# An adapter with a chosen expert ahead of a chosen feed-forward: the first block's bias, index reads, norm rows and idle products

## The chip, the cores and the metric

The kernel runs on one core of a Trainium2 chip. The metric is the device time of one execution in microseconds (us). Before the change it is 899.83 us, the median of three runs (899.83, 899.83 and 900.68). Engines are called as the profile calls them: PE is TensorE's matmul, PEld its weight load, DVE is VectorE, ACT is ScalarE, POOL is GpSimd, and SP is the sync engine, which here only reads indices and issues transfers.

## The reference

The input x is 2 sequences of 2048 tokens of width 512, in float32. Each sequence carries one index for each of two layers.

```python
# layer 1: adapter, one of 16 experts per sequence
hidden = gelu(x @ down_W.T + down_b)                 # 512 -> 128
hidden = where(valid, hidden @ expert_W[idx].T + expert_b[idx], hidden)
hidden = hidden + domain_emb[idx]
hidden = hidden @ up_W.T + up_b                      # 128 -> 512
x = layernorm(hidden + x) * ln_gamma + ln_beta
# layer 2: feed-forward, one of 8 experts per sequence
h = gelu(x @ Wi[e] + bi[e])                          # 512 -> 2048
x = layernorm(h @ Wo[e] + bo[e] + x) * gamma[e] + beta[e]
```

Nothing nonlinear stands between the chosen expert and the up projection, so the kernel folds the two matrices into one, and the three biases that follow the first gelu into one row of 512 values: `up_W @ (valid * expert_b + domain_emb) + up_b`.

## The kernel before, in words

The tokens are cut into 8 blocks of 512 (four per sequence), a block into four sub-tiles of 128 tokens; x lies in SBUF with tokens on the 128 partitions. For each block the adapter gives the normalized x and its transpose `yT`, `f_in` multiplies by Wi (2048 columns in four stages `d`) and applies gelu, and `f_out` multiplies by Wo, adds the residual and normalizes. Both large products are done in seven half-size products instead of eight (`mul` calls with sums of blocks that POOL and DVE prepare); only the very first stage of the first block, `pC`, is done plainly, in two halves, so that it can start when half of `yT` is there.

Every engine executes its instructions in the order in which the Python code writes them. There is no scheduler: later blocks' adapter work is put between products through hooks (`F` for `f_in`, numbered 0 to 27, and `G` for `f_out`), while the first block's adapter is written out by hand ahead of the loop (L668 to L706). A PSUM tile comes from small pools; the adapter's pieces share two "aux" buffers, so a piece must wait until what lies in its buffer has been read.

The parts that the change touches are these.

- L106 to L125: the first loads. SP issues the two index vectors and x's sub-tiles 0 and 1; ACT issues `down_W`, x's sub-tiles 2 and 3, `down_b`, `up_W`, and then three rows that are each copied to all 128 partitions: `up_b`, `ln_gamma`, `ln_beta`. The transfers of SP and ACT take eight semaphores in turn, and one that takes a semaphore again waits at its issue until the transfer that had it before has landed.
- L150 to L151: SP reads both sequences' indices for both layers, four reads, before it issues anything that uses one (`load_expert`, `load_wi` and the rest, L654 to L663).
- `fold_expert`, `fold_up`, `fold_bias`: the folding for a sequence. `fold_up` also makes `biasx`, the expert's bias vector repeated 128 times, by a product with ones and a copy by ACT. For the first block the bias comes in two parts: `a_residual(0)` lets POOL add `up_b` to x, and `a_up` adds `biasx` times the up projection by a second matmul into the same PSUM tile. For all other blocks `fold_bias` makes a full 128x512 tile of the whole bias once per sequence, and POOL adds it to x.
- L674: nine products of ones with ones (`keep_busy`) at the very start, into a PSUM tile that nobody reads.
- L682 to L706: the first block's order: all four transposes of x, two down projections, the transpose of up_W, the third down projection, the folding, the fourth, then `a_up` for sub-tiles 0 and 1, `a_norm`, the transpose of the expert's `bi`, `a_up` for 2 and 3, and the transposes into `yT` (`a_out`) for 0 and 1. `second_half` (L708) does the rest between the two halves of `pC`.
- L746 to L750: the second sequence's folding, at hooks 10, 17, 22 and 23 of the block before it.

Of the kernel before, what the change touches and what calls it, by code (L numbers as in the profile page):

```python
# [17 lines left out]
def kernel(  # L18
# [34 lines left out]
    P = 128  # L53
# [32 lines left out]
    def aux(name, pool=None, tag="aux"):  # L86
        return (pool or ps_a).tile([P, 512], F32, tag=tag, name=name)
# [24 lines left out]
    db = cpool.tile([A, 1], F32, name="db")  # L112
    g0 = cpool.tile([P, D], F32, name="g0")
    b0 = cpool.tile([P, D], F32, name="b0")
    upb = cpool.tile([P, D], F32, name="upb")
    nc.sync.dma_start(x_tiles[0][:, 0, :], xr[0][:, 0, :])
    nc.scalar.dma_start(dW, down_W)
    nc.sync.dma_start(x_tiles[0][:, 1, :], xr[0][:, 1, :])
# [1 line left out]
    nc.scalar.dma_start(x_tiles[0][:, 3, :], xr[0][:, 3, :])  # L120
    nc.scalar.dma_start(db, down_b.rearrange("(a o) -> a o", o=1))
    nc.scalar.dma_start(uW, up_W.rearrange("(c p) a -> p c a", p=P))
    nc.scalar.dma_start(upb, up_b.partition_broadcast(P))
    nc.scalar.dma_start(g0, ln_gamma.partition_broadcast(P))
    nc.scalar.dma_start(b0, ln_beta.partition_broadcast(P))  # L125

    ident = cpool.tile([P, P], F32, name="ident")
    make_identity(nc, ident)
    mhalf = cpool.tile([P, NS], F32, name="mhalf")
    nc.gpsimd.memset(mhalf, -0.5)  # L130

    tok_f = cpool.tile([1, 2, B], F32, name="tok_f")
    nc.vector.tensor_copy(tok_f, tok_i)
# [13 lines left out]
    flags = cpool.tile([1, 2, B], F32, name="flags")  # L147
    nc.vector.scalar_tensor_tensor(flags[:, 0, :], tok_f[:, 0, :], 0.0, below, ALU.is_ge, ALU.mult)
    nc.vector.tensor_scalar(flags[:, 1, :], flags[:, 0, :], -1.0, 1.0, ALU.mult, ALU.add)
    e0 = [nc.sync.value_load(e_i[0:1, 0, b : b + 1], min_val=0, max_val=E0 - 1) for b in range(B)]  # L150
    e1 = [nc.sync.value_load(e_i[0:1, 1, b : b + 1], min_val=0, max_val=E1 - 1) for b in range(B)]  # L151


    seq = [{} for _ in range(B)]
# [1 line left out]
    def load_expert(b):  # L156
        w = seq[b]
        w["eb"] = spool.tile([1, 2, A], F32, tag="eb", name=f"eb_{b}")
        nc.sync.dma_start(w["eb"][:, 0, :], expert_b[ds(e0[b], 1)])
        nc.sync.dma_start(w["eb"][:, 1, :], domain_emb[ds(e0[b], 1)])  # L160
        w["ew"] = spool.tile([A, A], F32, tag="ew", name=f"ew_{b}")
        nc.sync.dma_start(w["ew"], expert_W[ds(e0[b], 1)].rearrange("e o a -> (e o) a"))
# [11 lines left out]
    def fold_expert(b):  # L174

        w = seq[b]
        v, iv = flags_all[:, 0, b : b + 1], flags_all[:, 1, b : b + 1]
        row = spool.tile([1, A], F32, tag="ebias", name=f"ebias_{b}")
        nc.vector.scalar_tensor_tensor(row, w["eb"][:, 0, :], flags[:, 0, b : b + 1], w["eb"][:, 1, :], ALU.mult, ALU.add)

        eff = spool.tile([A, A], F32, tag="eff", name=f"eff_{b}")
        nc.vector.tensor_scalar(eff, ident, iv, None, ALU.mult)
        nc.vector.scalar_tensor_tensor(eff, w["ew"], v, eff, ALU.mult, ALU.add)
        w["ebias"], w["eff"] = row, eff

    def fold_up(b):
        w = seq[b]
        pw = aux(f"pw_{b}")
        nc.tensor.matmul(pw, w["eff"], uWT, start=True, stop=True)
        w["up"] = spool.tile([A, D], F32, tag="up", name=f"up_{b}")  # L190
        nc.scalar.copy(w["up"], pw)

        pe = aux(f"pe_{b}")
        nc.tensor.matmul(pe[:, :P], w["ebias"], ones[0:1, :], start=True, stop=True)
        w["biasx"] = spool.tile([A, P], F32, tag="biasx", name=f"biasx_{b}")
        nc.scalar.copy(w["biasx"], pe[:, :P])

    def fold_bias(b):
        w = seq[b]
        pb = aux(f"pb_{b}")  # L200
        nc.tensor.matmul(pb, w["biasx"], uWT, start=True, stop=False)
        nc.tensor.matmul(pb, ones[0:1, :], upb[0:1, :], start=False, stop=True)
        w["upb"] = spool.tile([P, D], F32, tag="upb", name=f"upb_{b}")
        nc.scalar.copy(w["upb"], pb)

# [10 lines left out]
    def load_wi(n, d):  # L216
        b = n // BPB
        t = wi_pool.tile([P, NC, 2, 2 * P], F32, tag="wi", name=f"wi_{n}_{d}")
        src = Wi[ds(e1[b], 1)].rearrange("e (c p) (r i) -> p (e c) r i", p=P, r=2)
        for r in range(2):  # L220
            nc.sync.dma_start(t[:, :, r, :], src[:, :, r, d * 2 * P : (d + 1) * 2 * P])
        wi_tiles[n, d] = [t]
# [71 lines left out]
    def a_transpose(n, s):  # L294
        if s == 0:
            live["xT"] = t_pool.tile([P, NC, TB], F32, tag="xyT", name=f"xT_{n}")
        transpose_subtile(x_tiles[n][:, s, :], live["xT"], s, f"x_{n}_{s}", n == 0)

    def a_down(n, lo, hi):

        xT = live["xT"]
        if lo == 0:
            live["hid"] = t_pool.tile([A, TB], F32, tag="hid", name=f"hid_{n}")
        t = slice(lo * P, hi * P)
        if n == 0:
            ph = aux(f"pdown_{n}_{lo}", *((ps_y, "Y") if lo % 2 else (ps_w, "W")))
        else:
            ph = aux(f"pdown_{n}")
        for c in range(NC):
            nc.tensor.matmul(ph[:, t], dWT[:, c, :], xT[:, c, t], start=(c == 0), stop=(c == NC - 1))  # L310
        nc.scalar.activation(live["hid"][:, t], ph[:, t], AF.Gelu, bias=db, scale=1.0)

    def a_residual(n):


        by = seq[n // BPB]["upb"] if n else upb
        for s in range(NS):
            nc.gpsimd.tensor_tensor(x_tiles[n][:, s, :], x_tiles[n][:, s, :], by, ALU.add)

    def a_up(n, s):  # L320
        w = seq[n // BPB]
        pu = aux(f"pup_{n}_{s}")
        nc.tensor.matmul(pu, live["hid"][:, ts(s, P)], w["up"], start=True, stop=(n > 0))  # L323
        if n == 0:
            nc.tensor.matmul(pu, w["biasx"], uWT, start=False, stop=True)
        r = x_tiles[n][:, s, :]
        nc.vector.tensor_add(r, pu, r)
        if s == 0:
            live["mv"] = moments_tile(f"a_{n}")
        moments(live["mv"], s, r, f"a_{n}_{s}")  # L330
        if n == 0:
            live["rstd", s] = rstds(live["mv"], s, s + 1, EPS0, f"a_{n}_{s}")
        elif s % 2:
            live["rstd", s] = live["rstd", s - 1] = rstds(live["mv"], s - 1, s + 1, EPS0, f"a_{n}_{s}")

    def a_norm(n, s):
        normalize(x_tiles[n][:, s, :], live["mv"], live["rstd", s], s, g0, b0)
# [313 lines left out]
        nc.sync.dma_start(outr[n][:, s, :], x_tiles[n][:, s, :])  # L651


    load_expert(0)  # L654
    load_wi(0, 0)
    load_bi(0)
    load_wi(0, 1)
# [21 lines left out]
    for c in range(NC):  # L679
        nc.tensor.transpose(pd[:, ts(c, P)], dW[:, ts(c, P)], ident)  # L680
    nc.vector.tensor_copy(dWT.rearrange("p c a -> p (c a)"), pd)
    for s in range(NS):  # L682
        a_transpose(0, s)
    a_residual(0)
    a_down(0, 0, 1)
    a_down(0, 1, 2)
    pu = aux("pt_uW")
    for c in range(NC):
        nc.tensor.transpose(pu[:, ts(c, P)], uW[:, c, :], ident)
# [2 lines left out]
    fold_expert(0)  # L692
    fold_up(0)
    a_down(0, 3, 4)
    a_up(0, 0)
    a_up(0, 1)
    a_norm(0, 0)
    fold_bi(0)
    a_norm(0, 1)
    a_up(0, 2)  # L700
    a_up(0, 3)
    sums_wi(0, 1)
    a_out(0, 0)
    a_out(0, 1)
    a_norm(0, 2)
    a_norm(0, 3)  # L706

# [13 lines left out]
    for n in range(NB):  # L721
        b, k = divmod(n, BPB)
        fresh = k == 0
        F = {i: [] for i in range(28)}
        for d in range(ND):
            if m := after(n, d, 3):
                F[7 * d + 6].append(lambda m=m: load_wi(*m))
            if m := after(n, d, 2):
                F[7 * d + 6].append(lambda m=m: sums_wi(*m))
        if fresh:  # L730
            for i in range(4):
                F[7 * i + 5].append(lambda i=i: sums_wo(b, i))
        if fresh and n:
            F[0].append(lambda: load_wo(b))
        if n:
            for s, i in enumerate((0, 1, 3, 4)):
                F[i].append(lambda s=s: f_moments(n - 1, s))
            F[4].append(lambda: f_rstd(n - 1, 0, NS))
            for s, i in enumerate((7, 8, 14, 15)):
                F[i].append(lambda s=s: f_normalize(n - 1, s))  # L740
                F[i + 3].append(lambda s=s: f_store(n - 1, s))
            if n + 1 < NB:
                F[19].append(lambda: load_x(n + 1))
            if fresh:
                F[19].append(lambda: (load_row(b, "gamma", gamma), load_row(b, "beta", beta)))
        if k == BPB - 1 and b + 1 < B:  # L746
            F[10].append(lambda: (load_expert(b + 1), load_bi(b + 1), load_row(b + 1, "bo", bo)))
            F[17].append(lambda: fold_expert(b + 1))
            F[22].append(lambda: fold_up(b + 1))
            F[23].append(lambda: fold_bias(b + 1))  # L750
        for d in range(ND - 1):
            F[7 * (d + 1) + 3].append(lambda d=d: h_s13(n, d))
        f_in(n, F)
        G = adapter_pieces(n + 1) if n + 1 < NB else {}
        if k == BPB - 1 and b + 1 < B:
            G[2].append(lambda: fold_bi(b + 1))
        f_out(n, G, n + 1 == NB)
# [34 lines left out]
```

## Time and profile before

| what | value |
|---|---|
| median of three runs | 899.83 us |
| the profiled execution: its time, its span | 902.11 us, 900.34 us |
| PE busy, share of the span | 883.6 us, 98% |
| PEld, DVE, ACT, POOL busy | 83%, 54%, 25%, 38% |
| mean granted TensorE clock | 0.993 |
| first product of `pC` starts | 33.82 us |
| last product ends | 893.83 us |
| moved from HBM | 53.37 MB read, 8.39 MB written |

The profile is of one execution, which took 2.28 us longer than the median; 1.77 us of its time lie outside the span of its instructions. Times in the views are microseconds from the start of the span. A row of the timeline has the start, the busy time, the engine, the line in the code, the operation with what it writes and reads, and in brackets the engine's idle time before it with what ended that. A row of the view by stretches has the stretch, then its length, each engine's busy time in it (with the number of instructions), the granted clock as a share of full speed, the busy share of the 16 transfer engines and the rate in GB/s. The chain of waits is followed back from the last instruction, and its time-ordered form lists the start, the time and the work.

### The profile page before, as it was taken

To read this page: it belongs to the slowest core of one execution; us is meant where nothing else is said; L and a number is where in the kernel's file an instruction comes from. 1 tells how busy PE (TensorE), PEld (TensorE's weight loads), DVE (VectorE), ACT (ScalarE), POOL (GpSimd) and SP (SyncE) were. 2 spreads that over 40 slices of the span, in tenths; PEclk is the share of its full clock that TensorE was granted. 3 is DMA by queue.
4 is the path that set the end of the run, shared out by engine and by line. 5 is a ranking of instruction groups with operands and counts; after the bars stand their busy time and mean duration, and the time that the engine had idled before them with its cause. 6 is when DMAs were issued, how large, how long until landed. Compare 5 with 4: busy or idle time off the path is not lost.

```text
span 900.3 us, 10433 instructions
## 1 busy us (share of the span) xinstructions
PE 883.6 (98%) x4054; PEld 747.2 (83%) x4054; DVE 485.0 (54%) x689; ACT 225.3 (25%) x463; POOL 339.7 (38%) x255
## 2 busy tenths in 40 slices
PE   7899999999999999999999999999999999999997
PEld 6588888887888878888788888888888887888876
DVE  2644374743657446663556746465374843556235
ACT  2134201431034301343013520144101540034200
POOL 2588511542224512344026970244411552224001
PEclk8899999999999999999999999999999999999999
DMA  9622100340013300251007610034000440011001
GB/s 269 248 87 67 36 0 1 129 152 1 1 46 122 113 1 1 66 183 48 1 1 257 187 47 1 1 117 142 22 1 1 140 141 1 0 47 47 1 1 47
DMA packets 46860, 62.42 MB, mean 69 GB/s; under 512 B 2360, under 2 KB 35932, under 8 KB 45916
## 3 DMA queue, kind: packets, MB, share of 16 engines
q1 hardware_dynamic: 45276, 59.93, 19.6%
q10 hardware_dynamic: 1536, 1.84, 0.8%
q8 instruction: 32, 0.52, 0.2%
q14 instruction: 16, 0.13, 0.1%
HBM read 53.37 MB, written 8.39 MB: 69 GB/s over the span
## 4 chain that ended last, share of the span: by engine, by line
PE 94%; DVE 1%; issue 1%; ACT 0%; POOLq 0%; POOL 0%; DVEq 0%; ACTq 0%
PE gX L384 18%; PE pX L384 18%; PE pZ L384 12%; PE gZ L384 12%; PE gW L384 6%; PE pW L384 6%; PE pY L384 6%; PE gY L384 6%; PE pdown L310 3%; PE pup L323 3%; PE pC L384 2%; PE pt_y L291 2%; PE pt_x L291 1%; DVE x L541 0%; DVE x L279 0%
## 5 line engine op out<-in xcount | busy, mean ns | idle before, releaser
L404 ACT ACTIVATE h<-c,biT 128x256 f32<-128x256 f32 x248 | 105.8, 497 | 76.4 <-DVE c L451 76.4
L384 PE MATMUL gX<-wo,h 128*128 128x256 f32 x512 | 115.6, 379 | 1.7 <-DVE x L541 1.7
L384 PE MATMUL pX<-yT,wi 128*128 128x256 f32 x496 | 117.2, 379 | 0.0
L384 PEld LDWEIGHTS gX<-wo,h 128*128 128x128 f32 x512 | 95.6, 190 | 14.1 <-DVE x L541 2.1
L384 PEld LDWEIGHTS pX<-yT,wi 128*128 128x128 f32 x496 | 94.2, 190 | 12.8
L447 ACT COPY c<-pX 128x512 f32<-128x512 f32 x93 | 54.0, 580 | 182.1 <-PE pX L384 182.1
L230 POOL TENSOR_TENSOR wis<-wi 128x512 f32<-128x512 f32 x31 | 41.2, 1329 | 131.7 <-PE pZ L384 131.7
L274 POOL TENSOR_TENSOR rstd_a<-ve_a,mhalf 128x2 f32<-128x2 f32 (+1 forms) x18 | 16.0, 887 | 186.2 <-DVE ve_a L272 186.2
L451 DVE TENSOR_TENSOR c<-pX,c 128x512 f32<-128x512 f32 x31 | 21.4, 691 | 112.0 <-ACT c L447 112.0
L292 ACT COPY yT<-pt_y 128x512 f32<-128x512 f32 x32 | 18.7, 587 | 225.2 <-PE pt_y L291 225.2
L541 DVE TENSOR_TENSOR x<-gX,x 128x512 f32<-128x512 f32 x32 | 21.4, 689 | 99.6 <-PE gX L384 99.5
L274 POOL TENSOR_TENSOR rstd_f<-ve_f,mhalf 128x4 f32<-128x4 f32 (+2 forms) x10 | 10.2, 1024 | 155.6 <-DVE ve_f L272 155.6
L508 DVE TENSOR_TENSOR s<-s,h 128x512 f32<-128x512 f32 x32 | 35.6, 1154 | 47.9 <-PE gZ L384 47.9
L347 POOL TENSOR_TENSOR x<-x,bo 128x512 f32<-128x512 f32 x32 | 41.0, 1284 | 53.2 <-PE pt_y L291 53.2
L384 PEld LDWEIGHTS gX<-wos,s 128*128 128x128 f32 x256 | 48.6, 190 | 13.2 <-issue 6.7
L384 PE MATMUL pZ<-yTs,wis 128*128 128x256 f32 x248 | 58.7, 379 | 0.0
L384 PE MATMUL pX<-yTs,wis 128*128 128x256 f32 x248 | 58.7, 379 | 0.0
L384 PEld LDWEIGHTS gZ<-wos,s 128*128 128x128 f32 x256 | 48.6, 190 | 12.1 <-issue 6.2
L384 PE MATMUL pW<-yTs,wi 128*128 128x256 f32 x248 | 58.6, 379 | 0.0
L384 PE MATMUL pY<-yT,wi 128*128 128x256 f32 x248 | 58.6, 379 | 0.0
L384 PE MATMUL pZ<-yT,wis 128*128 128x256 f32 x248 | 58.6, 379 | 0.0
L384 PE MATMUL gX<-wos,s 128*128 128x256 f32 x256 | 57.8, 379 | 0.3 <-DVE x L541 0.3
(114 smaller groups left out, 1541.4 us busy)
## 6 DMA issues: line engine op xcount, KB each, us to landing
wi<-in_L_cond_Wi_dram SPq DMA_DIRECT2D x64, 512.0 KB, 4.3
wo<-in_L_cond_Wo_dram SPq DMA_DIRECT2D x16, 512.0 KB, 10.0
out_dram<-x SPq DMA_DIRECT2D x32, 256.0 KB, 2.0
x<-in_x_dram SPq DMA_DIRECT2D x7, 1024.0 KB, 4.9
x<-in_x_dram SPq DMA_DIRECT2D x2, 256.0 KB, 4.0
x<-in_x_dram ACTq DMA_DIRECT2D x2, 256.0 KB, 5.1
bo<-in_L_cond_bo_dram SPq DMA_DIRECT2D x2, 256.0 KB, 7.6
gamma<-in_L_cond_gamma_dram SPq DMA_DIRECT2D x2, 256.0 KB
```

What stands on the lines that cost most here:

```text
L230: tt(s1, a21, a22, ALU.add)
L274: nc.gpsimd.tensor_tensor(rstd[:, lo:hi], ve[:, lo:hi], mhalf[:, lo:hi], ALU.pow)
L291: nc.tensor.transpose(pt[:, ts(c, P)], src[:, ts(c, P)], ident)
L310: nc.tensor.matmul(ph[:, t], dWT[:, c, :], xT[:, c, t], start=(c == 0), stop=(c == NC - 1))
L323: nc.tensor.matmul(pu, live["hid"][:, ts(s, P)], w["up"], start=True, stop=(n > 0))
L347: nc.gpsimd.tensor_tensor(r, r, seq[n // BPB]["bo"], ALU.add)
L384: nc.tensor.matmul(bank[:, q], lhsT(k, q), rhs(k, q), start=first, stop=True, skip_group_check=True)
L404: nc.scalar.activation(h[:, j, c * HT : (c + 1) * HT], pre[:, q], AF.Gelu, bias=w["bi"][:, j : j + 1], scale=1.0)
L447: nc.scalar.copy(t, src)
L451: nc.vector.tensor_add(t, src, t)
L508: nc.vector.tensor_tensor(t[:, i : i + 2], s1[:, i : i + 2], h_blocks(n, k, k + 2)[0], ALU.subtract)
L541: nc.vector.tensor_add(t, src, t)
```

## The change

`up_b` is loaded as one row of 512 values instead of 128 copies, and it, `ln_gamma` and `ln_beta` are issued from POOL's queue after its first memsets instead of from ACT's. SP reads one index at a time: the first sequence's adapter index, then its three adapter loads, then its feed-forward index; the second sequence's two reads move to hook 10.

The whole bias becomes one row. `fold_up` makes a column of the expert's bias (a matmul with one output column, copied by DVE), the new `fold_row` multiplies it by the up projection into one row of PSUM and DVE adds `up_b`. In the first block `a_up` adds that row by a matmul with ones instead of the `biasx` product, and POOL's four adds of `a_residual(0)` are gone. `fold_bias` spreads the row to 128 partitions by one matmul instead of two.

In the first block's order the transposes of x are mixed with the down projections, the transpose of `bi` moves behind `a_up` of sub-tile 3, and `keep_busy` products are put in at four places (6, 6, 2 and 2).

```diff
-    upb = cpool.tile([P, D], F32, name="upb")
+    upb = cpool.tile([1, D], F32, name="upb")
...
-    nc.scalar.dma_start(upb, up_b.partition_broadcast(P))
-    nc.scalar.dma_start(g0, ln_gamma.partition_broadcast(P))
-    nc.scalar.dma_start(b0, ln_beta.partition_broadcast(P))
-
     ident = cpool.tile([P, P], F32, name="ident")
     make_identity(nc, ident)
     mhalf = cpool.tile([P, NS], F32, name="mhalf")
     nc.gpsimd.memset(mhalf, -0.5)
+    nc.gpsimd.dma_start(upb, up_b.rearrange("(o d) -> o d", o=1))
+    nc.gpsimd.dma_start(g0, ln_gamma.partition_broadcast(P))
+    nc.gpsimd.dma_start(b0, ln_beta.partition_broadcast(P))
...
-    e0 = [nc.sync.value_load(e_i[0:1, 0, b : b + 1], min_val=0, max_val=E0 - 1) for b in range(B)]
-    e1 = [nc.sync.value_load(e_i[0:1, 1, b : b + 1], min_val=0, max_val=E1 - 1) for b in range(B)]
+    e0, e1 = {}, {}
+
+    def read_e0(b):
+        e0[b] = nc.sync.value_load(e_i[0:1, 0, b : b + 1], min_val=0, max_val=E0 - 1)
+
+    def read_e1(b):
+        e1[b] = nc.sync.value_load(e_i[0:1, 1, b : b + 1], min_val=0, max_val=E1 - 1)
...
-        row = spool.tile([1, A], F32, tag="ebias", name=f"ebias_{b}")
-        nc.vector.scalar_tensor_tensor(row, w["eb"][:, 0, :], flags[:, 0, b : b + 1], w["eb"][:, 1, :], ALU.mult, ALU.add)
         eff = spool.tile([A, A], F32, tag="eff", name=f"eff_{b}")
         nc.vector.tensor_scalar(eff, ident, iv, None, ALU.mult)
         nc.vector.scalar_tensor_tensor(eff, w["ew"], v, eff, ALU.mult, ALU.add)
+        row = spool.tile([1, A], F32, tag="ebias", name=f"ebias_{b}")
+        nc.vector.scalar_tensor_tensor(row, w["eb"][:, 0, :], flags[:, 0, b : b + 1], w["eb"][:, 1, :], ALU.mult, ALU.add)
...
         pe = aux(f"pe_{b}")
-        nc.tensor.matmul(pe[:, :P], w["ebias"], ones[0:1, :], start=True, stop=True)
-        w["biasx"] = spool.tile([A, P], F32, tag="biasx", name=f"biasx_{b}")
-        nc.scalar.copy(w["biasx"], pe[:, :P])
+        nc.tensor.matmul(pe[:, 0:1], w["ebias"], ones[0:1, 0:1], start=True, stop=True)
+        col = spool.tile([A, 1], F32, tag="ecol", name=f"ecol_{b}")
+        nc.vector.tensor_copy(col, pe[:, 0:1])
+        w["ecol"] = col
+
+    def fold_row(b):
+
+        w = seq[b]
+        pb = aux(f"pb_{b}")
+        nc.tensor.matmul(pb[0:1, :], w["ecol"], uWT, start=True, stop=True)
+        w["brow"] = spool.tile([1, D], F32, tag="brow", name=f"brow_{b}")
+        nc.vector.tensor_add(w["brow"], pb[0:1, :], upb)
 
     def fold_bias(b):
         w = seq[b]
-        pb = aux(f"pb_{b}")
-        nc.tensor.matmul(pb, w["biasx"], uWT, start=True, stop=False)
-        nc.tensor.matmul(pb, ones[0:1, :], upb[0:1, :], start=False, stop=True)
+        pb = aux(f"pbb_{b}")
+        nc.tensor.matmul(pb, ones[0:1, :], w["brow"], start=True, stop=True)
...
     def a_residual(n):
 
-
-        by = seq[n // BPB]["upb"] if n else upb
         for s in range(NS):
-            nc.gpsimd.tensor_tensor(x_tiles[n][:, s, :], x_tiles[n][:, s, :], by, ALU.add)
+            nc.gpsimd.tensor_tensor(x_tiles[n][:, s, :], x_tiles[n][:, s, :], seq[n // BPB]["upb"], ALU.add)
...
         if n == 0:
-            nc.tensor.matmul(pu, w["biasx"], uWT, start=False, stop=True)
+            nc.tensor.matmul(pu, ones[0:1, :], w["brow"], start=False, stop=True)
...
+    read_e0(0)
     load_expert(0)
+    read_e1(0)
     load_wi(0, 0)
...
-    for s in range(NS):
-        a_transpose(0, s)
-    a_residual(0)
+    a_transpose(0, 0)
+    a_transpose(0, 1)
     a_down(0, 0, 1)
+    a_transpose(0, 2)
     a_down(0, 1, 2)
+    a_transpose(0, 3)
...
     fold_up(0)
     a_down(0, 3, 4)
+    fold_row(0)
     a_up(0, 0)
     a_up(0, 1)
+    keep_busy(6)
     a_norm(0, 0)
-    fold_bi(0)
     a_norm(0, 1)
     a_up(0, 2)
     a_up(0, 3)
+    fold_bi(0)
     sums_wi(0, 1)
+    keep_busy(6)
     a_out(0, 0)
+    keep_busy(2)
     a_out(0, 1)
+    keep_busy(2)
     a_norm(0, 2)
     a_norm(0, 3)
...
-            F[10].append(lambda: (load_expert(b + 1), load_bi(b + 1), load_row(b + 1, "bo", bo)))
+            F[10].append(lambda: (read_e0(b + 1), read_e1(b + 1), load_expert(b + 1), load_bi(b + 1), load_row(b + 1, "bo", bo)))
             F[17].append(lambda: fold_expert(b + 1))
             F[22].append(lambda: fold_up(b + 1))
-            F[23].append(lambda: fold_bias(b + 1))
+            F[23].append(lambda: fold_row(b + 1))
+            F[24].append(lambda: fold_bias(b + 1))
```

## The prediction

> **What bounds the kernel now.** I read the chain of waits first. It is PE almost throughout:
>
> ```profile
> PE 94%; DVE 1%; issue 1%; ACT 0%; POOLq 0%; POOL 0%; DVEq 0%; ACTq 0%
> ```
>
> From about 53 us on PE never waits until the last block (828.1 us busy in the 830 between 60 and 890), and the diff leaves that work's products alone. So the change can act only through when the first feed-forward product `pC` starts (33.82 us), what PE does up to 53 us, and the seam between the sequences. The same chain in order of time, 28 to 60 us:
>
> ```profile
> 30.44 0.61 DVE x L327
> 31.09 0.67 PE pt_y L291 x4
> ...
> 33.82 8.87 PE pC L384 x32
> ...
> 44.08 1.12 PE pb L201 x2
> 45.21 1.05 PE pb L202 x2
> 46.26 7.10 PE pC L384 x32
> ```
>
> The same 32 passes of `pC` take 8.87 us, then 7.10; and `pC` stands behind DVE's add of sub-tile 2 (L327), whose PSUM buffer the transpose takes. The view by stretches, cut at the clock's changes, tells where the 1.77 us went:
>
> ```profile
> 6.90:10.30 3.40, 2.58 (x21) 2.04 (x20) 0.66 (x1) 1.85 (x4) 0.00 (x0) 1.00 0.87 157
> 13.70:17.10 3.40, 1.06 (x3) 0.31 (x3) 2.25 (x2) 0.00 (x0) 3.40 (x3) 1.00 1.10 352
> 17.10:20.50 3.40, 3.40 (x12) 2.68 (x12) 0.00 (x0) 1.22 (x3) 0.00 (x1) 0.51 1.08 355
> 20.50:24.00 3.50, 3.50 (x6) 1.41 (x5) 0.60 (x1) 0.00 (x0) 0.00 (x0) 0.50 1.07 369
> 30.80:34.20 3.40, 1.92 (x11) 1.20 (x11) 3.19 (x9) 1.17 (x2) 0.77 (x2) 1.00 1.06 411
> 34.20:37.60 3.40, 3.40 (x10) 2.69 (x9) 3.19 (x4) 0.00 (x0) 3.32 (x3) 0.50 0.71 272
> ```
>
> A stretch with 1.06 or 1.92 us of PE busy is followed by half clock; one with 2.58 is not. Half clock lasted two stretches from 17.1 us (small matmuls did not lift it) and one from 34.2. Last, the timeline up to the first add:
>
> ```profile
> 7.79 0.36 SPq L162 DMA_DIRECT2D ew<-in_L_cond_expert_W_dram  x1
> 8.20 1.07 ACT L292 COPY xT<-pt_x 128x512 f32<-128x512 f32 x2 [5.96 <-DMA upb<-in_L_cond_up_b_dram]
> 12.01 5.09 POOL L318 TENSOR_TENSOR x<-x,upb 128x512 f32<-128x512 f32 x4 [10.64 <-DMA eb<-n_L_cond_domain_emb_dram]
> 13.35 1.34 DVE L182 TENSOR_SCALAR eff<-ident,flags_all 128x128 f32<-128x128 f32 x1
> 14.73 1.25 DVE L183 SCALAR_TENSOR_TENSOR eff<-ew,flags_all,eff 128x128 f32<-128x128 f32 x1
> 16.04 1.12 PE L189 MATMUL pw<-uWT,eff 128*128 128x512 f32 x2 [2.94 <-DVE eff L183]
> 23.40 0.69 DVE L327 TENSOR_TENSOR x<-pup,x 128x512 f32<-128x512 f32 x1 [7.42 <-PE pup L325]
> ```
>
> ACT's copies wait for ACT's own row issues (to 8.15). DVE's two `eff` instructions take 2.6 us beside POOL's adds; the second sequence's take 0.27 and 0.35. PE waits 2.94 us for them, and that gap brings the half clock under which everything to the first add at 23.40 runs.
>
> [...]
>
> **The change, part by part.** T is the start of DVE's first add (23.40 before), with full-clock rates of this trace: four transposes 0.45, a down projection 0.94, a 512-column matmul 0.95.
>
> *Norm rows from POOL.* POOL is free at 1.4 us, so the rows' 512 KB are asked for near 2.5 us, not from 5.5. They now compete with x. The engines were full until 7.5, when x's sub-tile 1 let its transpose go (7.38). 256 packets of 2 KB at the 95 ns of such packets later in the trace are 1.5 us on 16 engines. Bounds: 0 if they come late, and about 3 if their slow spell comes too (9.0 to 10.5 us: 0.99 busy, 67 GB/s). I take 1.2: sub-tile 1 at 8.55. In exchange ACT's queue is free at about 6, since `uW`, which now waits for sub-tile 0 (5.5), is its last issue. `uW` lands near 10, PE asks for it after 12. `g0` and `b0` are asked for after 20 and `up_b`'s row after 16: hidden.
>
> *Index reads.* Three reads of 0.56 us leave SP's way to the adapter loads, but `ew` now waits at its issue for sub-tile 1's landing, so it goes out at about 8.6 instead of 7.8. It took 6.3 us among the three rows; without them I take 3, and DVE asks at about 13.5, or 15 with half clock. If it took 6 again, 1 us is lost. Behind it wait the Wi loads and everything else of SP, which landed by 17.2 for a need at 30 or later: hidden.
>
> *Residual adds gone, `eff` first.* 5.1 us of POOL that nobody awaits, but DVE's `eff` becomes 0.27 + 0.35 us.
>
> *Opening at full clock:* transpose 1 8.55, down 0 to 9.95, transpose 2 10.4, down 1 11.35, transpose 3 11.8, uW 12.25, DVE copy of it 13.1, `eff` 13.8, pw 14.8, pe 15.0, down 3 15.9, row product 16.9, up 17.8, DVE's row 17.7, bias 18.8, so T = 18.9. Only one matmul (row product) is added to this path; the bias matmul costs what the `biasx` one did.
>
> *But the clock.* The stretch from 6.9 to 10.3 now has 10.3 - 8.55 = 1.75 us of PE work, under the 1.92 that brought half clock. So half clock follows from 10.3: for one stretch the path loses 1.6 us (work in 3.4 us at half, less DVE's waits), for two 2.7. I take 2.1: **T = 21.0**, 2.4 us before 23.40.
>
> *From T to `pC`.* `bi`'s transpose now takes sub-tile 2's buffer, so `pt_y` waits for the add of sub-tile 3 instead of 2. That add ended at 32.77 = T + 9.37; biT's copy (0.16) leaves its way and sub-tile 1 comes 0.15 sooner: T + 9.05, so `pt_y` at T + 9.1 and `pC` 2.73 later (31.09 to 33.82), T + 11.85, against T + 10.42. **1.4 us is given back.** The idle products cost nothing at full clock: one is 0.23 us[...]. Six after sub-tile 1 end at T + 3.4, and the next up pair is needed at T + 6.6; six after `bi` (T + 7.3) end at T + 8.9, just ahead of `pt_y`; the twos fit into ACT's 0.7 us copies. At half clock the second six would end at T + 10.3, 1.2 us late. `pC` starts at 21.0 + 11.85 = 32.85: **1.0 us gained.**
>
> *Clock in `pC`.* The last 3.4 us ahead of it hold 0.6 + 0.94 us of idle products and 1.1 of transposes, 2.6, like the stretch that kept full clock: **1.77 us gained**; 0 if the threshold lies higher.
>
> *`fold_bias`* drops one of two matmuls on the chain (L202): **1.05 us gained.** The row is long there. POOL's sums start at about T + 10.2 and stay ahead of PE (ready T + 36.5, needed T + 44).
>
> *Second sequence.* pe 128 columns to 1, row product and spreading for the two old products: the same PE time within 0.2. The row waits on DVE's 0.16 us column copy, with 1.6 us of products between; DVE's queue holds one 0.69 us add there. SP's two reads at hook 10 (1.1 us) stand ahead of a Wi load needed 20 us later. Zero; +1 if DVE is late.
>
> Sum: 1.0 + 1.77 + 1.05 = 3.8 us. The profiled execution would go from 902.11 to 898.3; it was 2.28 above the median, so the median goes from 899.83 to about **896.0**.
>
> **Rivals.**
> - *Opening at full clock* (sub-tile 1 hardly delayed[...]): T = 18.9, or 17.7 without delay; 893.9 or 892.7. [...] Against: full transfer engines until 7.5.
> - *Half clock for three stretches, or rows much slower:* T near 23.3, so `pC` starts 1.4 late and the gain is 1.77 + 1.05 - 1.4 = 1.4: 898.4. For it: 17.1 to 20.5 had 3.40 us busy and was not lifted.
> - *The idle products don't hold the clock in `pC`:* 1.77 lost, twos and second six late by about 1.2: 896.0 + 3.0 = 899.0, no change.
> - *Slower: the rows block x.* Place: x's sub-tile 1 on the shared engines. Each us of its delay costs one on the path, beyond the 1.2 taken. With the forecast's 3.8 of gain it is slower by 0.2% once the landing is 5.6 us further off, past 14 us; at 15 the time is 902.5. For it: the three rows took from 5.5 to 14.3 us in this trace. Against: [...] plain 2 KB rows later took 95 ns.
>
> **How the numbers follow.** Forecast 0.37; full clock 0.28; three stretches 0.15; clock lost in `pC` 0.10; blocked 0.10. 0.2% of 899.83 is 1.8 us, about what a measurement can tell: faster means under 898.0. The first two are faster, of the next a third, and a fifth of the clock case, as its size is uncertain: 0.72, with 0.04 for parts of the blocked case too mild to count: 0.76. Same gets 0.15, slower 0.09. The range leaves out the quickest opening and the blocked case: 892.3 to 899.6.
>
> **What would show it.** Right: the first add (now L336) at 19 to 23 us; `eff` at 0.3 us each; the chain going through sub-tile 3's add into `pt_y`; 32 passes of `pC` at 7.1 us both times; one 1.05 us `pbb`. Wrong: sub-tile 1's transpose past 10 us or before 7.6; half clock in `pC`; DVE waiting for `ew` or the norm rows; a PE wait near 405 us.

## The result, and the profile after

| | before | after |
|---|---|---|
| median, the two kernels in turn on one chip (11 runs each) | 899.77 us | 896.44 us |
| lowest, highest run | 896.35, 900.68 us | 895.65, 900.22 us |
| profiled execution: time, span | 902.11, 900.34 us | 896.54, 894.78 us |
| first add (T) | 23.40 us | 17.32 us |
| first product of `pC` | 33.82 us | 30.79 us |
| first product of `pX` (end of the second `pC` pass) | 53.36 us | 47.59 us |

The ratio of after to before is 0.9970, with a 95% interval of 0.9957 to 0.9983: 3.3 us faster by the medians, more than the 0.2% (1.8 us) that the prediction took as measurable; the ends of the interval are gains of 1.5 and 3.9 us. The profiled pair shows 5.6 us, because the profiled execution of before was 2.3 us above its median and that of after on it.

The chain of waits of the changed kernel, as shares of the span:

```profile
PE 97%; DVE 1%; issue 1%; DMA 1%; ACT 0%; POOLq 0%; POOL 0%; SPq 0%; DVEq 0%; ACTq 0%
```

The same chain in order of time, up to 48 us:

```profile
1.85 4.53 DMA x<-in_x_dram
...
6.42 0.66 PE pt_x L302 x4
...
19.39 1.53 PE idle L679 x12
...
24.94 0.23 PE pt_bi L220
25.17 2.86 PE idle L679 x12
28.03 0.70 PE pt_y L302 x4
...
30.79 7.19 PE pC L393 x32
...
39.37 1.12 PE pbb L213 x2
40.48 7.10 PE pC L393 x32
```

Three things are to be seen. x's sub-tile 1 lands at 6.38 us and PE starts on it at once; before, its transpose started at 7.38. `pt_y` no longer waits for a DVE add but for PE itself, behind six idle products that take 2.86 us. Both passes of `pC` now take 7.1 to 7.2 us (before: 8.87 and 7.10), and one `pbb` product stands where two stood.

The view by stretches, cut at the clock's changes:

```profile
18.20:21.60 3.40, 3.40 (x17) 1.93 (x16) 2.95 (x8) 0.00 (x0) 0.83 (x2) 1.00 1.08 377
21.60:25.00 3.40, 3.40 (x8) 0.96 (x7) 3.17 (x6) 0.00 (x0) 0.72 (x1) 1.00 1.04 387
25.00:28.40 3.40, 3.40 (x16) 3.36 (x17) 3.23 (x9) 0.00 (x0) 1.11 (x2) 0.50 1.05 389
28.40:31.80 3.40, 2.89 (x20) 2.40 (x19) 3.19 (x4) 1.17 (x2) 3.32 (x3) 1.00 1.06 408
```

One half-clock stretch is left, from 25.0 to 28.4, and it lies under the six idle products. It came after a stretch in which PE was busy for all of its 3.40 us. That is what the prediction's reading of such stretches (little busy time, then half clock) could not give, and it was the first question for the experiments.

The timeline up to the first add:

```profile
6.34 0.59 ACT L303 COPY xT<-pt_x 128x512 f32<-128x512 f32 x1 [4.09 <-PE pt_x L302]
6.39 0.36 SPq L166 DMA_DIRECT2D ew<-in_L_cond_expert_W_dram  x1
10.99 0.28 DVE L184 TENSOR_SCALAR eff<-ident,flags_all 128x128 f32<-128x128 f32 x1
11.30 0.35 DVE L185 SCALAR_TENSOR_TENSOR eff<-ew,flags_all,eff 128x128 f32<-128x128 f32 x1
11.71 1.13 PE L193 MATMUL pw<-uWT,eff 128*128 128x512 f32 x2 [0.47 <-DVE eff L185]
17.32 0.69 DVE L336 TENSOR_TENSOR x<-pup,x 128x512 f32<-128x512 f32 x1 [1.43 <-PE pup L334]
```

ACT copies as soon as PE is done (6.34 us; before 8.20), `eff` takes 0.28 and 0.35 us, and no stretch between 6 and 25 us is at half clock. The three row transfers, issued by POOL at 1.50 to 2.75 us, did not begin to move data until 4.75 us (`up_b`) and 5.87 us (the two norm rows), and landed at 5.86, 7.87 and 8.79. Two issues waited as the prediction has it, each for the transfer that had its semaphore before: `ew` went out at 6.39, when sub-tile 1 had landed (6.38; SP waited 1.0 us), and `uW` at 4.96, when sub-tile 0 had (4.94).

### The profile page after: what moved, and what is told of

The parts are those of the page before. It is cut to its first block, busy times and chain, and to the rows that moved or that the text cites. A ratio compares the mean times of both kernels' runs of the same rounds, so it can differ in the third digit from the quotient of the medians.

```text
span 894.8 us, 10499 instructions
## 1 busy us (share of the span) xinstructions
PE 883.6 (99%) x4086; PEld 747.6 (84%) x4086; DVE 484.5 (54%) x693; ACT 224.6 (25%) x461; POOL 336.6 (38%) x254
## 3 DMA queue, kind: packets, MB, share of 16 engines
q10 hardware_dynamic: 1104, 1.05, 0.4%
## 4 chain that ended last, share of the span: by engine, by line
PE 97%; DVE 1%; issue 1%; DMA 1%; ACT 0%; POOLq 0%; POOL 0%; SPq 0%; DVEq 0%; ACTq 0%
PE gX L393 18%; PE pX L393 18%; PE pZ L393 12%; PE gZ L393 12%; PE gW L393 6%; PE pW L393 6%; PE pY L393 6%; PE gY L393 6%; PE pup L332 3%; PE pdown L321 3%; PE pC L393 2%; PE pt_x L302 2%; PE pt_y L302 2%; DMA x<-in_x_dram 1%; PE idle L679 0%
## 5 line engine op out<-in xcount | busy, mean ns | idle before, releaser
L460 DVE TENSOR_TENSOR c<-pX,c 128x512 f32<-128x512 f32 x31 | 21.4, 692 | 108.2 <-ACT c L456 108.2
L285 POOL TENSOR_TENSOR rstd_f<-ve_f,mhalf 128x4 f32<-128x4 f32 (+2 forms) x10 | 10.3, 1025 | 155.6 <-DVE ve_f L283 155.6
```

The lines of the kernel that those rows point to most:

```text
L285: nc.gpsimd.tensor_tensor(rstd[:, lo:hi], ve[:, lo:hi], mhalf[:, lo:hi], ALU.pow)
L460: nc.vector.tensor_add(t, src, t)
```

## The experiments

T is the start of the first add. Each run below was timed in turn with the kernel before, and the changed kernel in its own such comparison; the medians of before lie between 898.88 and 899.77 us in these comparisons. A difference of less than 1 us between two runs of different comparisons is therefore not certain by the medians alone. Each trace is of one execution.

### What the half clock follows

**One-row or 128-row bias matmul.** In the changed kernel the bias is added by a matmul whose two operands have one row each. The edit gives both 128 rows (127 rows of the bias operand are zero); the number of matmuls and their columns stay.

```diff
+    brow_all = cpool.tile([P, D], F32, name="brow_all")
+    nc.vector.memset(brow_all, 0.0)
...
-        w["brow"] = spool.tile([1, D], F32, tag="brow", name=f"brow_{b}")
+        w["brow"] = brow_all[0:1, :]
...
-            nc.tensor.matmul(pu, ones[0:1, :], w["brow"], start=False, stop=True)
+            nc.tensor.matmul(pu, ones, brow_all, start=False, stop=True)
```

> In the first block the bias row is added by a matmul over all 128 rows (127 of them zero) instead of over one row; everything else as in the changed kernel. Theory A (a matmul over one row doesn't count as work for the clock, so the half clock at 24.6 us comes from the four of them): no half clock between 15 and 45 us, the six idle products ahead of the transposes into yT take 1.5 us instead of 2.9, and the first product of pC starts about 12.2 us after DVE's first add instead of 13.5; the time is about 1.3 us under the changed kernel's (about 895.2). Theory B [...]: it still appears in the same place, 13.5 us, time as the changed kernel (896.4).

Measured: median 895.30 us, ratio to before 0.9964 (0.9952 to 0.9975), 1.1 us under the changed kernel; 17 of its 22 executions lie below the lowest of the changed kernel's 11 (895.65). The stretches of this kernel:

```profile
21.60:25.00 3.40, 2.62 (x9) 1.11 (x8) 3.26 (x5) 0.00 (x0) 0.23 (x1) 1.00 1.05 386
25.00:28.40 3.40, 3.12 (x27) 2.75 (x26) 3.12 (x10) 0.72 (x2) 1.60 (x3) 1.00 1.04 385
```

PE is busy for less of the same stretch (2.62 instead of 3.40 us), and yet the clock stays full after it. `pC` starts at T + 11.70 instead of T + 13.47. So it is not busy time alone that kept the clock here: matmuls over one row keep PE busy in the records and counted for less. A stretch of 3.4 us can hold more or less of them. Of the one-row products alone (L334), the stretches of the changed kernel from 14.77, 18.18 and 21.59 us hold

```profile
14.77:18.18 3.41, 1.12 (x2) 1.00 1.06 288
18.18:21.59 3.41, 1.12 (x2) 1.00 1.08 377
21.59:25.01 3.42, 2.24 (x4) 1.00 1.05 387
```

and only the last is followed by half clock. The same in all six profiles with one-row bias products: of the full-clock stretches in which PE was busy for 98% or more, five had 2.05 to 2.24 us of these products and were each followed by half clock, ten had 1.08 to 1.94 us and none was. One row doesn't count as nothing, though: with 1.94 us of it, 1.5 us of other work held the clock, less than the 1.92 that brought half clock in the prediction's profile. Nor is busy time a sharp limit without it: in the profile with eight POOL additions, below, a stretch with 1.84 us of PE busy was not followed by half clock. What exactly is counted isn't shown.

A second thing is seen in the spacing: with the 128-row bias product an up pair takes 1.72 us, with the one-row one 2.10. The profile with four POOL additions, which has one-row products and no half clock after T, parts the two: its `pC` starts at T + 12.09. So of the 1.77 us between T + 13.47 and T + 11.70, about 0.4 is the spacing and 1.4 the clock.

**Without the idle products**, in the changed kernel and in the 128-row one: the four added `keep_busy` lines are removed.

```diff
-    keep_busy(6)
     a_norm(0, 0)
...
-    keep_busy(6)
     a_out(0, 0)
-    keep_busy(2)
     a_out(0, 1)
-    keep_busy(2)
```

> The changed kernel without its four added groups of idle products (16 in all). If they hold the clock: the transposes into yT start about 1.2 to 1.6 us earlier, but the first half of pC or the up projections run at half clock for one stretch of 3.4 us or more, and the time is 896.4 to 898.5. If they only take time: pC starts about 1.6 us earlier (11.9 us after the first add), stays at full clock, and the time is about 894.9.

> The 128-row bias kernel (895.3) without the four added groups of idle products. Theory A (the idle products are needed only because the bias matmuls of one row lose the clock): the up pairs end near 22 at full clock, no half clock sets in between the first add and pC, pC's first passes take 7.1 to 7.2 us, and the median is 895 to 896.5. Theory B (the clock is lost while PE waits for DVE, whatever the bias matmul's rows): a half clock sets in ahead of or in pC, whose first passes take 8.5 to 10 us, and the median is 897.5 to 900, near the 900.0 of the changed kernel without idle products.

Measured: the changed kernel without them has a median of 900.04 us, ratio 1.0021 (1.0010 to 1.0032): a little slower than the kernel before, and slower than either expectation, since half clock lasted three stretches (25.8 to 36.0 us). The 128-row kernel without them has 898.61, ratio 0.9998 (0.9981 to 1.0015), 3.3 us above the same kernel with them. The stretches of the latter, and its chain in order of time:

```profile
21.90:25.30 3.40, 1.22 (x4) 0.29 (x2) 3.17 (x6) 0.00 (x0) 0.50 (x1) 1.00 1.05 387
25.30:28.70 3.40, 1.21 (x5) 0.82 (x6) 3.12 (x10) 0.59 (x1) 1.33 (x2) 0.52 1.04 386
28.70:35.50 6.80, 6.13 (x16) 4.74 (x17) 3.97 (x3) 0.59 (x1) 6.72 (x6) 0.50 0.94 364
```

```profile
28.60 1.13 PE pt_y L304 x4
...
30.39 9.78 PE pC L395 x32
```

While PE waits for DVE's adds and normalizations it is busy for 1.2 us in 3.4; under the half clock that follows the four transposes take 1.13 us instead of 0.66 (128-row kernel), and it lies over 5 us of `pC`. Here theory A, that 128-row bias matmuls make the idle products needless, fell: the idle products are needed because PE waits for DVE there, whatever the rows. They are worth 3.6 us in the changed kernel, more than the whole measured gain.

**The kernel before with the idle products alone**: the same four lines added to it.

> The kernel before with only the four groups of idle products added, at the places where the change has them. Theory A (they hold the clock between the up pairs and pC by themselves): the first pC pass takes 7.1 to 7.2 us in every profile, while the half clock ahead of the first add, which begins at the gap before pw, stays; the median is 0.9 to 1.8 us under the kernel before's 899.2: 897.4 to 898.3. Theory B (they pay only together with the change's other parts, since at half clock they last twice as long and are late): median within 0.5 us of 899.2 or above it, with pt_y waiting behind idle products.

Measured: 898.89 us, ratio 0.9998 (0.9983 to 1.0013): no difference that can be told. The profiled execution shows both halves of the reason:

```profile
29.12 1.34 PE idle L668 x12
30.45 0.44 PE pt_y L291 x4
...
32.45 7.19 PE pC L384 x32
```

`pC` ran at full clock, as theory A had it; but the sub-tile 2 add that frees `pt_y`'s buffer had ended at 29.13, so `pt_y` stood for 1.3 us behind idle products, as theory B had it. Its half clock lay ahead of T (8.7 to 15.5 us; T is 21.86), where these idle products can't help. So in this kernel they gave nothing that can be told.

**The kernel before, once more.**

> The kernel before, a second profile, to see which of its numbers repeat. The profiled execution of before took 902.1 us against a median of 899.8, so some of its half-clock stretches are expected to be shorter or missing here: first add between 20 and 23.4 us, pC between 30.5 and 33.8, sub-tile 1 of x landed at 7.0 to 7.6 us.

Measured: 898.04 us, span 896.3. Its stretches and its chain:

```profile
13.60:17.00 3.40, 1.75 (x6) 0.87 (x7) 1.56 (x2) 0.58 (x2) 1.14 (x1) 1.00 1.09 348
17.00:20.40 3.40, 3.40 (x11) 2.33 (x11) 0.00 (x0) 0.54 (x3) 0.00 (x0) 0.51 1.09 357
20.40:23.80 3.40, 2.75 (x7) 0.89 (x5) 2.32 (x5) 0.00 (x0) 0.45 (x1) 0.99 1.07 378
```

```profile
31.43 7.19 PE pC L384 x32
...
40.01 1.12 PE pb L201 x2
41.14 1.05 PE pb L202 x2
42.19 7.10 PE pC L384 x32
```

Here half clock follows a stretch with 1.75 us of PE busy, as the prediction read it, but it lasts one stretch instead of two, and `pC` keeps full clock with no idle products. Both half-clock stretches, this one and the one from 17.1 us in the prediction's profile, have PE busy throughout. They differ in a one-row product that lies inside the latter only:

```profile
17.09 0.78 PE L194 MATMUL pe<-ones,ebias 1*128 1x128 f32 x2
```

The other profiles fit that. Of the 20 half-clock stretches up to 45 us in all of them, 13 were filled with work that has no one-row product, and full clock followed each; six were busy for 1.3 to 2.7 us, and half clock followed each; the one from 17.1 us is the twentieth. That the one row is the cause there rests on this one case.

So two of the losses that the prediction's profile showed, 1.7 us in `pC` and about 2 us before T, are not in every execution of before. The 51 executions of before that ran beside the 128-row kernel spread from 895.5 to 902.2 us, while 19 of that kernel's 22 lie between 894.5 and 895.8. Against the second profile of before, the changed kernel's gains 1.5 us: 0.64 up to the start of `pC`, and 1.07 in `pbb`, less 0.2 later.

### What holds `pt_y`

The first edit, on the 128-row kernel, moves the transpose of `bi` back to where it stood before the change. The second gives the transposes of sub-tiles 0 and 1 two PSUM buffers that nothing else uses then, puts the transpose of `bi` behind them and drops the second six idle products.

```diff
     a_norm(0, 0)
+    fold_bi(0)
     a_norm(0, 1)
     a_up(0, 2)
     a_up(0, 3)
-    fold_bi(0)
```

> The 128-row bias kernel with bi's transpose put back to where it stood before the change (after the first normalization), so that pt_y takes the PSUM buffer that the add of sub-tile 2 frees instead of that of sub-tile 3. Theory A (the buffer of the add sets pt_y, as the prediction's step from T to pC says): pt_y starts right after the second six idle products, near T + 8.0 instead of T + 9.0, pC near T + 10.7 instead of T + 11.7, and the median is about 1.0 us under the 128-row kernel's 895.3: 894.3, ratio near 0.995. Theory B (DVE's normalizations or ACT set pt_y, whatever the buffer): pC stays at T + 11.7 and the median within 0.3 of 895.3.

```diff
-        transpose_subtile(x_tiles[n][:, s, :], live["yT"], s, f"y_{n}_{s}")
+        transpose_subtile(x_tiles[n][:, s, :], live["yT"], s, f"y_{n}_{s}", pool=((ps_w, "W"), (ps_y, "Y"))[s] if n == 0 and s < 2 else None)
...
-    fold_bi(0)
-    sums_wi(0, 1)
-    keep_busy(6)
     a_out(0, 0)
     keep_busy(2)
     a_out(0, 1)
     keep_busy(2)
+    fold_bi(0)
+    sums_wi(0, 1)
```

> The 128-row bias kernel with the transposes of sub-tiles 0 and 1 in two PSUM buffers that nothing else uses then, bi's transpose after them and the second six idle products left out. Theory A (only the buffer holds pt_y back, and what pC gains stays gained): pt_y of sub-tile 0 starts where the up products end (about 23.7 us, T + 6.5), pC near 26.0 (T + 8.8) at full clock, 2.9 us before the 128-row kernel, and the median is about 892.4, ratio near 0.993. Theory B (it is given back: POOL's sums, the transposes of sub-tiles 2 and 3 or a half clock then hold PE between pC and 55 us): a wait of PE of 1 to 3 us there and a median of 894.5 to 895.5.

Measured: 893.92 us, ratio 0.9957 (0.9941 to 0.9974), for the early `bi`; 892.38 us, ratio 0.9940 (0.9918 to 0.9961), for the own buffers. Both bear out theory A. The chains in order of time, first of the early `bi`, then of the own buffers:

```profile
24.44 1.34 PE idle L681 x12
25.78 0.44 PE pt_y L304 x4
...
27.77 7.19 PE pC L395 x32
```

```profile
24.13 0.86 PE pup L336 x2
24.98 0.44 PE pt_y L304 x4
...
26.98 7.19 PE pC L395 x32
```

With T at 17.20 in the first and 18.53 in the second, `pC` starts at T + 10.57 and T + 8.45, against T + 11.70 in the 128-row kernel. In the first, the add of sub-tile 2 ended at 24.46, and `pt_y` then stood behind idle products until 25.78. With its own buffer, `pt_y` follows the last up pair without a wait, though the add of sub-tile 3 starts only at 26.77. Nothing is given back later: PE runs on to 60 us as in the other kernels. What the buffers and what the six dropped idle products gave wasn't measured apart. The second one beats both kernels: its median is 6.5 us under that of before in the same comparison (898.88) and 4.1 under the changed kernel's 896.44.

### What moved the first add

**The rows back on ACT's queue**, in the changed kernel:

```diff
+    nc.scalar.dma_start(upb, up_b.rearrange("(o d) -> o d", o=1))
+    nc.scalar.dma_start(g0, ln_gamma.partition_broadcast(P))
+    nc.scalar.dma_start(b0, ln_beta.partition_broadcast(P))
...
-    nc.gpsimd.dma_start(upb, up_b.rearrange("(o d) -> o d", o=1))
-    nc.gpsimd.dma_start(g0, ln_gamma.partition_broadcast(P))
-    nc.gpsimd.dma_start(b0, ln_beta.partition_broadcast(P))
```

> The changed kernel with up_b's row, ln_gamma and ln_beta issued from ACT's queue as before. If the move to POOL pays by freeing ACT's queue: ACT's first copy of a transposed sub-tile waits until about 8 us (6.3 in the changed kernel), the first add comes 1 to 2 us later than 17.3, and the time is about 898. If the place of these loads doesn't matter: within 0.5 us of the changed kernel (896.4).

Measured: 898.04 us, ratio 0.9985 (0.9973 to 0.9998), 1.6 us above the changed kernel. The timeline:

```profile
7.36 0.66 PE L302 MATMUL pt_x<-ident,x 128*128 128x128 f32 x4 [0.92 <-DMA x<-in_x_dram]
7.97 0.44 ACTq L125 DMA_DIRECT2D b<-in_L_cond_ln_beta_dram  x1
8.45 1.07 ACT L303 COPY xT<-pt_x 128x512 f32<-128x512 f32 x2 [6.21 <-DMA uW<-in_L_cond_up_W_dram]
```

ACT makes its first copy at 8.45 us, after its last issue, and T is 19.43, 2.1 us later than with the rows on POOL's queue. (The profiled execution took 900.13 us, 2.1 above this kernel's median; half clock lay over both groups of six idle products.) Part of that is x itself: sub-tile 1 landed at 7.31 here. That landing is not fixed. In the four profiles with the rows on ACT's queue it came at 7.1 to 8.2 us; in the nine with the change's rows on POOL's, at 6.3 to 6.6 (five of them), 7.2 (two), 7.9 and 8.8. In the last two, 15 of the transfer's 16 parts had landed by 6.3 us and one came 1.8 and 2.5 us later. Why isn't settled. The later issue of `uW` alone does not explain it: in the run with all index reads first, below, `uW` went out at 2.97 us, as before the change, and sub-tile 1 landed at 6.32. Nor does it take a transfer of POOL's: in the kernel before with idle products, where POOL issues none, sub-tile 1 landed at 8.15.

**All index reads first**, in the changed kernel (the second sequence's two leave hook 10):

```diff
-    read_e0(0)
+    for b in range(B):
+        read_e0(b)
+    for b in range(B):
+        read_e1(b)
     load_expert(0)
-    read_e1(0)
```

> The changed kernel with all four index reads ahead of the first indexed load, as before the change. Theory A (the reads are hidden, since ew waits for x's sub-tile 1 anyway): eb goes out near 6.2 instead of 4.5, ew near 7.2 instead of 6.4 and lands by about 10.6, before DVE asks at 11.3; first add at 17.3 and the median within 0.3 us of the changed kernel's 896.4. Theory B (the reads are what brought ew early enough): eff's second instruction waits for ew, first add and median 0.5 to 1.5 us later.

Measured: 896.74 us, ratio 0.9989 (0.9975 to 1.0004), 0.3 above the changed kernel, within what can be told. T is 17.42 (17.32). `ew` went out at 7.24 us and DVE's second `eff` instruction still started at 11.39, right after the first. The reads are hidden.

**POOL's additions beside `eff`**: additions into a spare buffer that nothing reads, at the place of the removed residual additions, first four, then eight.

```diff
+    spare = t_pool.tile([P, NJ, TB], F32, tag="h", name="spare")
+    for s in range(NS):
+        nc.gpsimd.tensor_tensor(spare[:, s, :], x_tiles[0][:, s, :], g0, ALU.add)
```

> The changed kernel with four 128x512 additions on POOL (sub-tile of x plus gamma's row into a spare buffer that nothing reads) at the place of the removed residual additions, from about 8 to 13 us. Theory A (POOL's additions made DVE's eff slow): eff takes 1.2 to 1.4 us for each of its two instructions instead of 0.28 and 0.35, pw starts about 2 us later, PE has a gap of over 2 us there, and the median is 2 (clock held) to 4 us (half clock after the gap) above the changed kernel's 896.4: 898.4 to 900.4. Theory B (eff was slow for another reason, such as the landing rows): eff stays at 0.3 us each and the median within 0.3 of 896.4.

> The changed kernel with eight additions of 128x512 on POOL into a spare buffer instead of e8's four, from about 8.3 to 18 us, so that they overlap eff even when x lands late. Theory A (POOL's additions slow eff): both eff instructions take 1.2 to 1.4 us. Theory B: 0.28 and 0.35 us as in the changed kernel, with POOL busy beside them.

The four gave a median of 897.42 us, ratio 0.9996 (0.9977 to 1.0014), and no verdict on `eff`: x's sub-tile 1 landed at 8.78 in the profiled execution, so that the additions were over by 13.3 and `eff`, at 14.86, took 0.28 and 0.35 us. The eight (one execution, 898.31 us) overlap it. The timeline:

```profile
8.19 9.94 POOL L701 TENSOR_TENSOR spare<-x,g 128x512 f32<-128x512 f32 x8 [4.90 <-DMA g<-in_L_cond_ln_gamma_dram]
12.04 1.25 DVE L185 SCALAR_TENSOR_TENSOR eff<-ew,flags_all,eff 128x128 f32<-128x128 f32 x1
13.21 1.34 DVE L187 SCALAR_TENSOR_TENSOR ebias<-eb,flags 1x128 f32<-1x128 f32 x1
13.35 1.13 PE L193 MATMUL pw<-uWT,eff 128*128 128x512 f32 x2 [1.51 <-DVE eff L185]
```

These DVE instructions take as long as one of POOL's (9.94 / 8 is 1.24 us), even `ebias` with its one row of 128 values; the first, `eff` at 11.59, came through in 0.41. The second profile of before shows the edge: `eff` at 13.47, beside POOL's additions, takes 1.34 us, and the one at 14.85, after they ended at 14.73, 0.35. Not every DVE instruction is slowed. Beside the same eight additions, those that read PSUM took 0.69 (the copy of `uWT`), 0.16 (`ecol`) and 0.68 us (`brow`), as long as in the changed kernel. In that kernel's whole trace the 124 additions that read a PSUM tile at L460 take 0.68 to 0.69 us, whether POOL is busy or not, and its 64 second steps of normalization (L290), which read SBUF, 0.75 us where POOL stood idle (24 of them) and 0.75 to 1.75, with a median of 1.64, beside POOL's work (38). So in these traces the slowed instructions have their operands in SBUF; why they wait isn't shown. The changed kernel shows the same at 29.27, where a normalization takes 1.76 us instead of 0.74 beside POOL's sums.

**The old bias**, in the changed kernel:

```diff
-    upb = cpool.tile([1, D], F32, name="upb")
+    upb = cpool.tile([P, D], F32, name="upb")
...
-    nc.gpsimd.dma_start(upb, up_b.rearrange("(o d) -> o d", o=1))
+    nc.gpsimd.dma_start(upb, up_b.partition_broadcast(P))
...
-            nc.tensor.matmul(pu, ones[0:1, :], w["brow"], start=False, stop=True)
+            nc.tensor.matmul(pu, w["biasx"], uWT, start=False, stop=True)
...
+    a_residual(0)
     pu = aux("pt_uW")
```

> The changed kernel with the bias as before: up_b's row spread to 128 partitions by GpSimd's queue, residual additions on POOL in the first block, the biasx product in the up pairs, and two matmuls to spread it in fold_bias; queues, order, reads and idle products as changed. Theory A (POOL's additions slow eff; one-row matmuls bring the second half clock, and here are none in the up pairs): eff takes about 1.3 us each, pw starts some 2 us later, the row product's 0.95 us is gone, T is 18.3 with the clock held and up to 21 if the gap before pw brings half clock; the second six idle products take 1.6 us and pC starts at T + 11.7, so at 30.0 to 32.7 instead of 30.8; the spreading takes 1.05 us more. Median 896.7 to 899.4. Theory B (eff was slow for another reason): eff 0.3 us each, T near 16.4, pC near 28.1, median near 894.8.

Measured: 897.77 us, ratio 0.9996 (0.9981 to 1.0011), 1.3 us above the changed kernel and inside theory A's span, but by another way than it said. In the profiled execution x's sub-tile 1 landed at 9.2 us, half clock lay over 7.9 to 14.7 us, and POOL's additions, which wait for x's transposes, hardly met `eff` (0.36 and 0.35 us). T was 21.50. From there it went as theory A said: no half clock, six idle products in 1.53 us, `pC` at T + 11.70, and two spreading products of 2.1 us. So the run confirms the second part, the clock without one-row matmuls, and says nothing on `eff`.

Its opening shows something else, which bears on the prediction:

```profile
9.22 1.11 PE L294 MATMUL pt_x<-ident,x 128*128 128x128 f32 x4 [2.91 <-DMA x<-in_x_dram]
```

Here not one part of sub-tile 1 was late but all 16: they landed from 7.67 to 9.17 us, in the changed kernel from 5.89 to 6.38. The first transfer in POOL's queue was `up_b` in 128 copies (256 KB) instead of one row (2 KB). Its data moved from 4.71 us on, while x was still on its way, and all of it had landed at 7.46. So rows from POOL's queue seem to have delayed x here, by 2.8 us against the changed kernel (9.17 and 6.38), more than the prediction's 1.2; the one-row `up_b` would then be what keeps them out of its way there. This is read from one execution.

Not tried alone were the new order of x's transposes and down projections, and the second sequence's folding.

## Why the prediction came near, step by step

The forecast of 896.0 us met 896.44, within its range of 892.3 to 899.6, and the direction was right. Its steps did less well than its sum.

| step | predicted | measured (profiled pair) |
|---|---|---|
| x's sub-tile 1 delayed by the rows | 1.2 us later, 8.55 | 1.0 us earlier, 6.38 |
| half clock in the opening | 2.1 us lost, T = 21.0 | none, T = 17.32 |
| T to `pC` | 11.85 us | 13.47 us |
| clock in `pC` | 1.77 us gained | 1.68 us gained |
| `fold_bias` | 1.05 us gained | 1.07 us gained |
| index reads, second sequence | 0 | the rest of the run, from 48 us on, 0.2 us longer |

*The delay of x* was the step that failed first. It was put at 1.2 us, from the bandwidth of 512 KB asked for near 2.5 us. The rows were issued then, but the norm rows' data moved only from 5.87 us on, when sub-tile 1 was nearly in. The prediction had carried the lower bound ("0 if they come late"), and that is what happened. From `up_b`'s issue to its first data 3.3 us passed, from gamma's 3.7; no transfer of POOL's in the trace of before could have told it.

*The opening's half clock* followed from that delay by the prediction's own working: 1.75 us of PE work in the stretch from 6.9 to 10.3. With x at 6.38 the stretch was full and the clock held. So the rival "opening at full clock", with T at 17.7 without delay, is what the trace shows (17.32); the 0.28 that it was given was the author's estimate. The later steps of that chain held where its first came true: in the two profiles with x at 8.78 (four POOL additions) and 9.17 (old bias) half clock set in at 9.2 and 7.9 us, and T was 21.25 and 21.50, close to the 21.0 of the forecast. How the 6.1 us of T in the profiled pair divide is not measured: 2.0 are absent in the second profile of before; the rest is shared by the earlier x, ACT's copies, `eff` and the order.

*From T to `pC`* the prediction had both terms and mis-sized one. `bi`'s transpose made `pt_y` wait for the later buffer: priced at 1.4 us; with it moved back `pC` came 1.13 sooner, and then stood behind idle products. The second six idle products were free "at full clock", and "1.2 us late" at half: they were at half clock. The prediction's sum took full clock there; but of the 3.4 us of PE work ahead of them about 2.1 were one-row products. With 128 rows the same six take 1.3 to 1.5 us instead of 2.9, that is 0.22 to 0.26 each, near the 0.23 that was the estimate, and `pC` starts at T + 11.70, close to the 11.85 that was worked out.

*`pC`, `fold_bias`, the reads and the second sequence* came out as worked out, within 0.3 us. The idle products hold the clock in `pC`, as the two kernels without them show (9.8 us instead of 7.2), which also rules out the rival in which they don't. The slower rival, rows that block x, did not come: even the latest landing seen, 9.2 us, is far from its 14.

*Why the sum was near all the same.* In the profiled pair the steps give 6.1 (T) - 3.1 (T to `pC`) + 1.7 + 1.1 = 5.8 us, of which 5.6 are in the spans; the forecast had 3.8. But the forecast took its 3.8 us off the median of before, as if the median execution held the same losses as the profiled one, which lay 2.3 us above it. The second profile of before shows that it needn't: 1.7 us of `pC`'s loss and part of the opening's were absent there. So a gain 1.8 us too small in the profiled pair was set off by 2.3 us that the median could not lose. That the two errors nearly cancelled is luck, and the single profile could not have told it.

The executions of before show what the median gain consists of. The 144 that were timed beside the experiments differ mainly in their mean granted clock: the 40 with 0.998 or 0.999 took 895.4 to 897.0 us, the 52 with 0.995 had a median of 899.8, the 18 with 0.993 one of 901.3. The changed kernel's 11 lie between 895.65 and 900.22. Its quickest are no quicker than those of before: as far as these times show, what it changes is how much half clock a usual execution meets.

What stays open: how much one-row work counts for the clock, what makes one part of x's transfer late, and how the gain up to T divides.

## What to carry to other kernels

Ask of each stretch of PE work not only how long PE is busy but with what: here a stretch with 2.1 us of one-row matmuls was full and the clock fell after it, while a stretch with 2.6 us of 128-row work kept it; padding the row with zeros gave 1.1 us. Idle products paid here where PE waited for another engine (3.6 us) and cost time where a product was ready behind them (1.3 us); the better repair is the wait itself, here a shared PSUM buffer, and with two spare ones six of the sixteen idle products could go. And take an execution's clock losses off the median only after seeing them in a second execution.

## What the runs showed of the hardware beyond that

- A full-clock stretch of 3.4 us with PE fully busy was followed by half clock when 2.05 us or more of it were one-row matmuls (five stretches), and not with 1.94 or less (ten). An up pair with a one-row product takes 2.10 us instead of 1.72.
- At half clock, a stretch filled with work that has no one-row product was followed by full clock each time (13), one busy for 2.7 us or less never (six).
- In the changed kernel, transfers issued by POOL moved their first data 3.3 to 3.7 us after the issue.
- Beside POOL's additions, DVE instructions that read only SBUF took as long as one addition (1.25 to 1.34 us; one took 0.41), even for one row of 128 values; those that read PSUM were not slowed (0.68 us).
